# A graph-attention layer on one core: the order of the last blocks' work, and the queue of a path that does not run

## The chip, the core and the metric

The kernel runs on one core of a Trainium2 chip. A core has five engines that run side by side, each from its own queue of instructions: TensorE (matrix products, transposes), VectorE (elementwise work, maxima, searches), ScalarE (activation functions, copies), GpSimd (elementwise work, and here the gathers) and SyncE (starts transfers). Sixteen DMA engines move data between the main memory and the core. Engines and transfers meet in semaphores: an instruction waits until a semaphore has reached a number, and raises another when it is done. The metric is the device's time for one execution in microseconds, the median of several runs. All data are 32-bit floats.

## The reference, cut to what matters

```python
def _L0_gnn_ref(h, adj_mat, W, a):
    N_HEADS, N_HIDDEN, SLOPE = 4, 512, 0.01
    N = h.shape[0]                                             # 4096
    ht = (h @ W).reshape(N, N_HEADS, N_HIDDEN).transpose(1, 0, 2)
    a_src = a[:, :N_HIDDEN, 0]
    a_dst = a[:, N_HIDDEN:, 0]
    src = jnp.einsum('hnd,hd->hn', ht, a_src)
    dst = jnp.einsum('hnd,hd->hn', ht, a_dst)
    e = jax.nn.leaky_relu(src[:, :, None] + dst[:, None, :], SLOPE) + adj_mat[None]
    att = jax.nn.softmax(e, axis=-1)
    h_prime = jnp.einsum('hij,hjd->hid', att, ht)
    return h_prime.mean(axis=0)

x = _layernorm(x + _L0_gnn_ref(x, adj, L0_gnn_W, L0_gnn_a), axis=-1)   # eps 1e-5
```

`x` is 4096 x 512, `adj` 4096 x 4096 (64 MiB), `W` 512 x 2048. The entries of `adj` that are not zero lie between 0.05 and 1e9. They are added to scores of ordinary size, so the softmax of nearly every row is 1 at the row's largest entry of `adj` and 0 elsewhere. Then the attention's result for the row is that one row of `x`, times the mean of the four heads' weights.

## The kernel before

The kernel takes that short way for all rows (`leading_rows`), and beside it tests whether every row's largest entry leads the second by enough. The number of rows for which it doesn't goes into `any_bad`; if it is over zero, a general path computes those blocks in full. With these inputs it is zero, and each engine jumps over the general path at the end.

```python
HINTED = tuple(getattr(mybir.EngineType, name) for name in ("PE", "Activation", "DVE", "Pool"))
# ...
    leading_rows(tc, x, adj, W, a, out, ident, v, n_bad, any_bad)

    flag = nc.values_load(any_bad[0:1, 0:1], min_val=0, max_val=N)
    with tc.If(flag > 0, preferred_fallthrough_block=True, label="general"):
        general(tc, x, adj, W, out, ident, v, n_bad)
```

The 4096 rows are 32 blocks (`NB`) of 128. Each block's rows of `adj` (2 MiB) are loaded, VectorE finds the largest of every 64 entries, then the largest of those and its place; a gather fetches the 64 entries, VectorE finds the column among them, and a second gather fetches that row of `x`. TensorE transposes the gathered rows (`turn`) and multiplies them with the mean weights (`products`); the sum with `x` is normalised by row and stored. `Q` is 4, `LATE` is 28 and `BEHIND` is 24; the `x` rows of blocks 24 to 31 are loaded last, so blocks 24 to 27 get theirs added late (`add_x`). All tasks stand in the program in the order in which each engine runs them.

```python
        nc.vector.max_index(col, top[:, ib, :], adj_t[ib])
        gather_rows(ib, col)

    def turn(ib):
# ...
        tp = psum.tile([P, KB, P], F32, name="tp", bufs=2)
        for kb in range(KB):
            nc.tensor.transpose(tp[:, kb, :], y[:, ts(kb, P)], ident)
        yt = yt_of[ib] = rows.tile([P, KB, P], F32, name="yt")
        nc.scalar.copy(yt, tp)

# ...
    def add_x(engine, ib):
        engine.tensor_add(hold[:, ib, :], hold[:, ib, :], o_ps["by"][:, ib - BEHIND, :])
        o_ps[ib] = hold[:, ib, :]
# ...
    def store(queue, lo, n):
        queue.dma_start(out_rows[:, ds(lo, n), :], hold[:, ds(lo, n), :])
# ...
    def bound(part):

        if part == 0:
            xm = once.tile([P, 1], F32, name="xm")
            nc.vector.tensor_reduce(xm, xx, axis=AX.X, op=OP.max)
            px = of_bound[0] = psum.tile([1, P], F32, name="px", bufs=1)
            nc.tensor.transpose(px, xm, ident)
        elif part == 1:
            nc.vector.tensor_reduce(xg, of_bound[0], axis=AX.X, op=OP.max)
            nc.scalar.activation(xg, xg, AF.Sqrt)
            pb = of_bound[1] = psum.tile([P, 1], F32, name="px", bufs=1)
            nc.tensor.matmul(pb, ones[0:1, :], xg, start=True, stop=True)
        else:
            nc.vector.tensor_mul(lead_by, of_bound[1], vn)
            nc.vector.tensor_scalar(lead_by, lead_by, 1.05, 110.0, op0=OP.mult, op1=OP.add)
# ...
    def test():
        a1 = top[:, :, 0]
        nc.vector.tensor_tensor(gap, top[:, :, 1], inner[:, :, 1], op=OP.max)
        size = once.tile([P, NB], F32, name="size")
        nc.vector.scalar_tensor_tensor(size, a1, -1.0, a1, op0=OP.mult, op1=OP.max)
        nc.vector.tensor_sub(gap, a1, gap)
        nc.vector.tensor_scalar(size, size, -(2.0 ** -22), lead_by, op0=OP.mult, op1=OP.subtract)
        nc.vector.scalar_tensor_tensor(gap, gap, 0.9999, size, op0=OP.mult, op1=OP.add)
        nc.vector.tensor_scalar(gap, gap, 0.0, None, op0=OP.is_gt)

    def count():
        pg = psum.tile([1, NB], F32, name="px", bufs=1)
        nc.tensor.matmul(pg, ones[:, 0:1], gap, start=True, stop=True)
        return pg

    def report(pg):
        nc.vector.tensor_scalar(n_bad, pg, -1.0, float(P), op0=OP.mult, op1=OP.add)
        total = once.tile([1, 1], F32, name="total")
        nc.vector.tensor_reduce(total, pg, axis=AX.X, op=OP.add)
        nc.vector.tensor_scalar(any_bad, total, -1.0, float(N), op0=OP.mult, op1=OP.add)
```

`bound` finds from the largest row norm of `x` how much the first entry has to lead by, `test` compares, `count` adds over the partitions and `report` writes `n_bad` and `any_bad`. `moments` takes mean and variance on VectorE and the root on ScalarE, `factor` the reciprocal, `normalise` the last step on VectorE. `stats`, `rstd` and `finish` do the same on ScalarE and GpSimd.

The loop over the blocks, cut to what the change touches, and the work behind it:

```python
    for t in range(NB):
        if t == NB // 2:
            tc.mark_branch_hint_location("general", engines=HINTED)
        # ... loads, segment maxima, find_column(t - 2)
        if t == NB - 1:
            for ib in (BEHIND, LATE, BEHIND + 2, LATE + 2):
                load_x(ib, 2)
            row_norm(BEHIND)
            row_norm(BEHIND + 1)
            add_x(nc.gpsimd, BEHIND)
        find_segment(t)
        # ... turn(t - 3), products(t - 3), statistics

    row_norm(BEHIND + 2)
    row_norm(BEHIND + 3)
    row_norm(LATE)
    store(nc.sync, 0, Q)
    for ib in range(Q, BEHIND, 2):
        store(nc.sync, ib, 2)
    find_column(NB - 2)
    add_x(nc.gpsimd, BEHIND + 1)
    find_column_in_row(NB - 1)
    add_x(nc.gpsimd, BEHIND + 2)
    turn(NB - 3)
    products(NB - 4, KB - 1, KB)
    residual(NB - 3)
    products(NB - 3)
    for ib in range(LATE + 1, NB):
        row_norm(ib)
    stats(BEHIND)
    moments(LATE)
    bound(0)
    for ib in range(BEHIND, NB):
        find_inner(ib)
    factor(LATE)
    normalise(LATE, o_ps.pop(LATE))
    turn(NB - 2)
    residual_in_halves(NB - 1)
    products(NB - 2, 0, 1)
    bound(1)
    add_x(nc.vector, LATE - 1)
    stats(BEHIND + 1)
    moments(LATE - 1)
    products(NB - 2, 1, KB - 1)
    rstd(slice(BEHIND, BEHIND + 2))
    stats(BEHIND + 2)
    bound(2)
    test()
    pg = count()
    rstd(slice(BEHIND + 2, BEHIND + 3))
    moments(NB - 3)
    factor(LATE - 1, shift=True)
    report(pg)
    factor(NB - 3)
    normalise(NB - 3, o_ps.pop(NB - 3))
    turn(NB - 1)
    finish(BEHIND)
    finish(BEHIND + 1)
    products(NB - 2, KB - 1, KB)
    products_of_half(NB - 1, 0)
    products_of_half(NB - 1, 1)
    nc.vector.tensor_add(hold[:, NB - 2, :], o_ps[NB - 2], hold[:, NB - 2, :])
    o_ps[NB - 2] = hold[:, NB - 2, :]
    moments(NB - 2)
    stats_of_half(NB - 1, 0)
    factor(NB - 2)
    normalise(NB - 2, o_ps.pop(NB - 2))
    finish(BEHIND + 2)
    finish(BEHIND + 3)
    stats_of_half(NB - 1, 1)
    moments(NB - 1)
    factor(NB - 1, shift=True)
    finish_in_halves(NB - 1)
    for ib, n in ((NB - 4, 1), (NB - 3, 1), (BEHIND, 2), (NB - 2, 1), (BEHIND + 2, 2)):
        store(nc.sync, ib, n)
    store(nc.sync, NB - 1, 1)
```

The general path's transfers, all on GpSimd's queue:

```python
        for g in range(NCH):        # 8
            nc.gpsimd.dma_start(x_sb[:, ts(g, Q), :], x_blocks[:, ts(g, Q), :])
        for kb in range(KB):        # 4
            nc.gpsimd.dma_start(w_sb[:, kb, :], w_blocks[:, kb, :])
        # ...
    def block(ib):                  # for each block with a row that does not lead
        # ...
        nc.gpsimd.dma_start(adj_t, adj[ds(ib, P, NB), :])
        # ...
        nc.gpsimd.dma_start(r, x[ds(ib, P, NB), :])
        # ...
        nc.gpsimd.dma_start(out[ds(ib, P, NB), :], r)
```

Of the kernel before, what the change touches and what calls it, by code (L numbers as in the profile page):

```python
# [16 lines left out]
SLOPE = 0.01  # L17
EPS = 1e-5
LOWEST = -3.4028234663852886e38
HINTED = tuple(getattr(mybir.EngineType, name) for name in ("PE", "Activation", "DVE", "Pool"))  # L20
P = 128
C = 512
E = 64
# [43 lines left out]
def leading_rows(ctx, tc, x, adj, W, a, out, ident, v, n_bad, any_bad):  # L67
# [184 lines left out]
    def finish(ib):  # L252
        i = slice(ib, ib + 1)
        nc.scalar.activation(hold[:, ib, :], o_ps.pop(ib), AF.Identity, bias=nm[:, i], scale=sd[:, i])  # L254
# [50 lines left out]
    def store(queue, lo, n):  # L305
        queue.dma_start(out_rows[:, ds(lo, n), :], hold[:, ds(lo, n), :])
# [56 lines left out]
        elif part == 1:  # L363
            nc.vector.tensor_reduce(xg, of_bound[0], axis=AX.X, op=OP.max)
            nc.scalar.activation(xg, xg, AF.Sqrt)
            pb = of_bound[1] = psum.tile([P, 1], F32, name="px", bufs=1)
            nc.tensor.matmul(pb, ones[0:1, :], xg, start=True, stop=True)
        else:
            nc.vector.tensor_mul(lead_by, of_bound[1], vn)
            nc.vector.tensor_scalar(lead_by, lead_by, 1.05, 110.0, op0=OP.mult, op1=OP.add)  # L370

    gap = once.tile([P, NB], F32, name="gap")
# [27 lines left out]
    for t in range(NB):  # L400
# [13 lines left out]
        if t == NB - 1:  # L414
            for ib in (BEHIND, LATE, BEHIND + 2, LATE + 2):
                load_x(ib, 2)
            row_norm(BEHIND)
            row_norm(BEHIND + 1)
            add_x(nc.gpsimd, BEHIND)
        find_segment(t)  # L420
        if t < 2:
            mean_of_heads(t)
# [28 lines left out]
    row_norm(BEHIND + 2)  # L451
    row_norm(BEHIND + 3)
    row_norm(LATE)
    store(nc.sync, 0, Q)
    for ib in range(Q, BEHIND, 2):
        store(nc.sync, ib, 2)
    find_column(NB - 2)
    add_x(nc.gpsimd, BEHIND + 1)
    find_column_in_row(NB - 1)
    add_x(nc.gpsimd, BEHIND + 2)  # L460
    turn(NB - 3)
    products(NB - 4, KB - 1, KB)
    residual(NB - 3)
    products(NB - 3)
    for ib in range(LATE + 1, NB):
        row_norm(ib)
    stats(BEHIND)
    moments(LATE)
    bound(0)
    for ib in range(BEHIND, NB):  # L470
        find_inner(ib)
    factor(LATE)
    normalise(LATE, o_ps.pop(LATE))
    turn(NB - 2)
    residual_in_halves(NB - 1)
    products(NB - 2, 0, 1)
    bound(1)
    add_x(nc.vector, LATE - 1)
    stats(BEHIND + 1)
    moments(LATE - 1)  # L480
    products(NB - 2, 1, KB - 1)
    rstd(slice(BEHIND, BEHIND + 2))
    stats(BEHIND + 2)
    bound(2)
    test()
    pg = count()
    rstd(slice(BEHIND + 2, BEHIND + 3))
    moments(NB - 3)
    factor(LATE - 1, shift=True)
    report(pg)  # L490
    factor(NB - 3)
    normalise(NB - 3, o_ps.pop(NB - 3))
    turn(NB - 1)
    finish(BEHIND)
    finish(BEHIND + 1)
    products(NB - 2, KB - 1, KB)
    products_of_half(NB - 1, 0)
    products_of_half(NB - 1, 1)
# [3 lines left out]
    stats_of_half(NB - 1, 0)  # L502
    factor(NB - 2)
    normalise(NB - 2, o_ps.pop(NB - 2))
    finish(BEHIND + 2)
    finish(BEHIND + 3)
    stats_of_half(NB - 1, 1)
    moments(NB - 1)
# [8 lines left out]
def general(ctx, tc, x, adj, W, out, ident, v, n_bad):  # L517
# [20 lines left out]
    with ExitStack() as pre:  # L538
# [1 line left out]
        two = pre.enter_context(tc.tile_pool(name="two", bufs=2))  # L540
        pps = pre.enter_context(tc.tile_pool(name="pps", bufs=2, space=bass.MemoryType.PSUM))
        for g in range(NCH):
            nc.gpsimd.dma_start(x_sb[:, ts(g, Q), :], x_blocks[:, ts(g, Q), :])
        for kb in range(KB):
            nc.gpsimd.dma_start(w_sb[:, kb, :], w_blocks[:, kb, :])
        for g in range(NCH):
            xT = two.tile([P, KB, C], F32, name="xT")
            for q in range(Q):
# [26 lines left out]
    def block(ib):  # L575
# [1 line left out]
        nc.vector.tensor_copy(src_i, src[:, ds(ib, 1), :].rearrange("p o h -> p (o h)"))  # L577
        held = psum.tile([P, D], F32, name="o_ps", bufs=1)
        adj_t = score.tile([P, N], F32, name="adj_g")
        nc.gpsimd.dma_start(adj_t, adj[ds(ib, P, NB), :])  # L580
        for h in range(H):
            s = score.tile([P, N], F32, name="s")
            nc.scalar.activation(s, dst_b[:, h, :], AF.Identity, bias=src_i[:, h : h + 1])
# [33 lines left out]
                    start=(h == 0 and kb == 0), stop=(h == H - 1 and kb == KB - 1),  # L617
                )
        r = turned.tile([P, D], F32, name="y_g")
        nc.gpsimd.dma_start(r, x[ds(ib, P, NB), :])  # L620
        nc.vector.tensor_add(r, r, held)
        st = stat.tile([P, nc.vector.BN_STATS_DIM], F32, name="st_g")
        nc.vector.bn_stats(st, r)
# [4 lines left out]
        nc.scalar.activation(sd, sd, AF.Sqrt)  # L628
        nc.vector.reciprocal(sd, sd)
        nc.vector.tensor_scalar(r, r, mv[:, 0:1], sd, op0=OP.subtract, op1=OP.mult)  # L630
        nc.gpsimd.dma_start(out[ds(ib, P, NB), :], r)

    with tc.For_i(0, NB, 1) as ib:
        of_block = stat.tile([1, 1], I32, name="of_block", bufs=1)
# [32 lines left out]
```

## Time and profile before

| | |
|---|---|
| time, median of 3 runs | 242.43 us (242.37 to 242.82) |
| span of the profiled run | 240.8 us |
| granted TensorE clock | 0.965 |
| busy: TensorE, VectorE, ScalarE, GpSimd | 83%, 78%, 46%, 42% |
| moved by the DMA engines | 97.73 MB, mean 406 GB/s |
| SyncE's transfers | 88.8% of the DMA engines' span |
| the gathers' transfers | 10.0% |

The span runs from the first to the last recorded instruction; the time on the device is 1.6 us longer. In the profile PE is TensorE, PEld its weight loads, DVE VectorE, ACT ScalarE, POOL GpSimd and SP SyncE; a q behind a name is that engine's queue of control instructions. L208 is line 208 of the kernel. A line of groups shows what is written and read, how often, and the mean time of one; a chain of waits is followed back from the last instruction. The lines that carry the argument are shown in the prediction, under its first heading.

### The profile page before, as it was taken

Reading aid. Unit: us, or ns where it says so; the run is one execution under the profiler, and the core shown is the slowest. Engines: PE = TensorE matmul, PEld = TensorE weight load, DVE = VectorE, ACT = ScalarE, POOL = GpSimd, SP = SyncE. Lnnn points to the kernel's source line nnn. Section 1 sums busy time; section 2 is a strip of 40 time slices with the busy share of each in tenths; the row PEclk is TensorE's granted clock in tenths of the full one; section 3 lists DMA queues with packets and bytes.
Section 4 is the critical chain, followed back from the end, with each engine's and each line's share of the span. In section 5 each row is a group of like instructions: output and inputs, shape, how many; then the busy total and the mean of one; then the engine's idle time right before and its main releaser. Section 6 shows DMA issues by size and latency. Waiting matters only on the chain.

```text
span 240.8 us, 2519 instructions
## 1 busy us (share of the span) xinstructions
PE 199.2 (83%) x683; PEld 102.4 (43%) x683; DVE 186.9 (78%) x308; ACT 111.7 (46%) x267; POOL 100.8 (42%) x215
## 2 busy tenths in 40 slices
PE   0188958999999999999969879597878979979890
PEld 0035426556666655555424334242324433324460
DVE  2635785489869895989589969888799899988682
ACT  2012003035575757575747455446464645157571
POOL 1112322314627362646352753454364564567120
PEclk9999799589999999999999999999997999999997
DMA  6999999999999999999999999999999999999995
GB/s 242 442 419 416 423 429 411 424 416 411 431 410 423 404 425 420 412 413 422 419 423 416 414 422 416 420 407 426 411 430 396 400 398 403 402 410 417 413 385 210
DMA packets 14849, 97.73 MB, mean 406 GB/s; under 512 B 2280, under 2 KB 2280, under 8 KB 9968
## 3 DMA queue, kind: packets, MB, share of 16 engines
q1 hardware_dynamic: 11232, 88.09, 88.8%
q0 software_dynamic: 3584, 9.44, 10.0%
q8 instruction: 6, 0.10, 0.2%
q14 instruction: 11, 0.09, 0.1%
q10 hardware_dynamic: 16, 0.02, 0.0%
HBM read 89.15 MB, written 8.39 MB: 405 GB/s over the span
## 4 chain that ended last, share of the span: by engine, by line
DMA 72%; PE 10%; DVE 6%; issue 4%; POOL 3%; ACT 1%; SPq 1%; POOLq 0%
DMA adj_t<-in_adj_dram 44%; DMA hold<-in_x_dram 18%; PE o L221 5%; DVE seg L158 5%; DMA hold<-in_L_gnn_W_dram 3%; DMA y<-in_x_dram,col 3%; DMA lead<-in_adj_dram,row 3%; PE o L263 1%; PE o L214 1%; PE pv L335 1%; POOL y L181 1%; DVE col L201 1%; SPq L113 1%; PE tp L208 1%; POOL lead L171 1%
## 5 line engine op out<-in xcount | busy, mean ns | idle before, releaser
L158 DVE TENSOR_REDUCE seg<-adj_t 128x32 f32<-128x2048 f32 (+1 forms) x74 | 146.3, 1987 | 38.5 <-DMA adj_t<-in_adj_dram 38.1
L221 PE MATMUL o<-w_sum,yt 128*128 128x512 f32 x248 | 118.2, 618 | 0.7 <-ACT yt L210 0.7
L221 PEld LDWEIGHTS o<-w_sum,yt 128*128 128x128 f32 x248 | 45.7, 196 | 55.1 <-issue 44.0
L210 ACT COPY yt<-tp 128x512 f32<-128x512 f32 x32 | 18.8, 588 | 44.3 <-PE tp L208 38.3
L171 POOL DMA_INDIRECT lead<-in_adj_dram,row x32 | 32.3, 1008 | 14.1 <-POOL row L169 14.1
L181 POOL DMA_INDIRECT y<-in_x_dram,col x32 | 30.8, 963 | 15.7 <-POOL col L195 14.6
L208 PE MATMUL tp<-ident,y 128*128 128x128 f32 x128 | 19.7, 277 | 15.5 <-DMA y<-in_x_dram,col 15.5
L311 PE MATMUL o<-hold,ident 128*128 128x512 f32 x32 | 18.7, 737 | 15.7 <-DMA hold<-in_L_gnn_W_dram 15.7
L214 PE MATMUL o<-hold,ident 128*128 128x512 f32 x52 | 27.7, 615 | 1.2 <-DMA hold<-in_x_dram 1.2
L208 PEld LDWEIGHTS tp<-ident,y 128*128 128x128 f32 x128 | 14.3, 141 | 28.9 <-issue 27.5
L195 POOL TENSOR_TENSOR col<-start,within 128x1 uint32<-128x1 uint32 x31 | 5.9, 189 | 48.0 <-DVE within L193 48.0
L329 ACT COPY wt<-tp 128x512 f32<-128x512 f32 x16 | 9.2, 588 | 35.7 <-PE tp L327 35.7
L169 POOL TENSOR_TENSOR row<-at,first 128x1 uint32<-128x1 uint32 x32 | 6.0, 188 | 38.3 <-DVE at L167 38.3
L228 ACT ACTIVATE sq<-hold 128x512 f32<-128x512 f32 x32 | 19.8, 621 | 4.3 <-DMA hold<-in_x_dram 4.3
L335 PEld LDWEIGHTS pv<-at_d,wt 128*128 128x128 f32 x128 | 17.2, 200 | 7.3 <-ACT wt L329 3.7
L311 PEld LDWEIGHTS o<-hold,ident 128*128 128x128 f32 x32 | 7.3, 239 | 24.8 <-POOL row L169 11.0
L254 ACT ACTIVATE hold<-o,nm,sd 128x512 f32<-128x512 f32 x24 | 17.3, 775 | 0.0
L312 ACT ACTIVATE w_sum<-o 128x512 f32<-128x512 f32 x4 | 2.4, 598 | 31.8 <-PE o L311 31.8
L245 ACT ACTIVATE sq<-o,nm 128x512 f32<-128x512 f32 x24 | 16.5, 689 | 0.8
L335 PE MATMUL pv<-at_d,wt 128*128 128x2 f32 x128 | 16.0, 249 | 0.6 <-ACT wt L329 0.6
L243 ACT ACTIVATE sq<-o 128x512 f32<-128x512 f32 x24 | 14.7, 611 | 0.0
L327 PEld LDWEIGHTS tp<-ident,hold 128*128 128x128 f32 x64 | 7.9, 142 | 6.9 <-issue 6.9
(85 smaller groups left out, 137.3 us busy)
## 6 DMA issues: line engine op xcount, KB each, us to landing
adj_t<-in_adj_dram SPq DMA_DIRECT2D x27, 2048.0 KB
adj_t<-in_adj_dram SPq DMA_DIRECT2D x20, 512.0 KB
hold<-in_x_dram SPq DMA_DIRECT2D x6, 1024.0 KB
out_dram<-hold SPq DMA_DIRECT2D x12, 512.0 KB
hold<-in_L_gnn_W_dram SPq DMA_DIRECT2D x4, 1024.0 KB
hold<-in_x_dram SPq DMA_DIRECT2D x4, 512.0 KB
out_dram<-hold SPq DMA_DIRECT2D x1, 1024.0 KB
out_dram<-hold SPq DMA_DIRECT2D x4, 256.0 KB
```

The lines of the kernel that those rows point to most:

```text
L158: nc.vector.tensor_reduce(seg_of[ib][:, ts(k, S // n)], adj_t[ib][:, ts(k, N // n)].rearrange("p (s e) -> p s e", e=E), axis=AX.X, op=OP.max,)
L171: nc.gpsimd.indirect_dma_start(out=lead, out_offset=None, in_=adj_segs, in_offset=bass.IndirectOffsetOnAxis(ap=row[:, :1], axis=0),)
L181: nc.gpsimd.indirect_dma_start(out=y, out_offset=None, in_=x, in_offset=bass.IndirectOffsetOnAxis(ap=col[:, :1], axis=0),)
L208: nc.tensor.transpose(tp[:, kb, :], y[:, ts(kb, P)], ident)
L210: nc.scalar.copy(yt, tp)
L214: nc.tensor.matmul(o_ps[ib], ident, hold[:, ib, :], start=True, stop=False)
L221: nc.tensor.matmul(o_ps[ib], yt_of[ib][:, kb, :], w_sum[:, kb, :], start=(start and kb == 0), stop=(kb == KB - 1),)
L228: nc.scalar.activation(sq, hold[:, ib, :], AF.Square, accum_out=xx[:, ib : ib + 1])
L245: nc.scalar.activation(sq, o, AF.Square, bias=nm[:, i], accum_out=sd[:, i])
L254: nc.scalar.activation(hold[:, ib, :], o_ps.pop(ib), AF.Identity, bias=nm[:, i], scale=sd[:, i])
L311: nc.tensor.matmul(o, ident, hold[:, w_at + kb * H + h, :], start=(h == 0), stop=(h == H - 1))
L335: nc.tensor.matmul(pv[:, kb, h : 2 * H : H], wt[:, k, :], at_d[:, k, h : 2 * H : H], start=(k == 0), stop=(k == KB - 1),)
```

## The change

It does four things. The last tasks of the five engines get another order: the bound and the test come earlier against the work of the last four blocks, and one addition on GpSimd is moved behind a gather. The stores of the first 24 blocks are cut otherwise: ten of two blocks and then one of four, where one of four came first. The general path's transfers go to SyncE's queue instead of GpSimd's. And SyncE is told of the branch over the general path ahead of time, as the four other engines are. It is for an earlier end of the test and of the last block, and for a GpSimd queue without transfers in the general path.

```diff
-HINTED = tuple(getattr(mybir.EngineType, name) for name in ("PE", "Activation", "DVE", "Pool"))
+HINTED = tuple(getattr(mybir.EngineType, name) for name in ("PE", "Activation", "DVE", "Pool", "SP"))
@@ bound(part)
             nc.scalar.activation(xg, xg, AF.Sqrt)
-            pb = of_bound[1] = psum.tile([P, 1], F32, name="px", bufs=1)
+        elif part == 2:
+            pb = of_bound[2] = psum.tile([P, 1], F32, name="px", bufs=1)
             nc.tensor.matmul(pb, ones[0:1, :], xg, start=True, stop=True)
         else:
-            nc.vector.tensor_mul(lead_by, of_bound[1], vn)
+            nc.vector.tensor_mul(lead_by, of_bound[2], vn)
@@ the loop, t == NB - 1
             row_norm(BEHIND + 1)
-            add_x(nc.gpsimd, BEHIND)
         find_segment(t)
@@ behind the loop
-    store(nc.sync, 0, Q)
-    for ib in range(Q, BEHIND, 2):
+    for ib in range(0, BEHIND - Q, 2):
         store(nc.sync, ib, 2)
+    store(nc.sync, BEHIND - Q, Q)
     find_column(NB - 2)
+    add_x(nc.gpsimd, BEHIND)
     add_x(nc.gpsimd, BEHIND + 1)
     find_column_in_row(NB - 1)
     add_x(nc.gpsimd, BEHIND + 2)
     turn(NB - 3)
     products(NB - 4, KB - 1, KB)
     residual(NB - 3)
-    products(NB - 3)
+    products(NB - 3, 0, KB - 1)
     for ib in range(LATE + 1, NB):
         row_norm(ib)
     stats(BEHIND)
     moments(LATE)
     bound(0)
+    products(NB - 3, KB - 1, KB)
     for ib in range(BEHIND, NB):
         find_inner(ib)
+    bound(1)
     factor(LATE)
     normalise(LATE, o_ps.pop(LATE))
     turn(NB - 2)
     residual_in_halves(NB - 1)
-    products(NB - 2, 0, 1)
-    bound(1)
+    bound(2)
+    products(NB - 2, 0, 2)
+    bound(3)
+    test()
+    pg = count()
+    products(NB - 2, 2, KB - 1)
     add_x(nc.vector, LATE - 1)
     stats(BEHIND + 1)
+    stats(BEHIND + 2)
     moments(LATE - 1)
-    products(NB - 2, 1, KB - 1)
     rstd(slice(BEHIND, BEHIND + 2))
-    stats(BEHIND + 2)
-    bound(2)
-    test()
-    pg = count()
     rstd(slice(BEHIND + 2, BEHIND + 3))
+    report(pg)
+    turn(NB - 1)
     moments(NB - 3)
     factor(LATE - 1, shift=True)
-    report(pg)
     factor(NB - 3)
     normalise(NB - 3, o_ps.pop(NB - 3))
-    turn(NB - 1)
-    finish(BEHIND)
-    finish(BEHIND + 1)
+    for ib in range(BEHIND, BEHIND + 3):
+        finish(ib)
     products(NB - 2, KB - 1, KB)
@@ ... normalise(NB - 2), then
-    finish(BEHIND + 2)
     finish(BEHIND + 3)
@@ general(), and the same in its four other transfers
-            nc.gpsimd.dma_start(x_sb[:, ts(g, Q), :], x_blocks[:, ts(g, Q), :])
+            nc.sync.dma_start(x_sb[:, ts(g, Q), :], x_blocks[:, ts(g, Q), :])
```

More of the change, by code (lines that the diff above doesn't have):

```diff
@@ L542, in general @@
         for g in range(NCH):
-            nc.gpsimd.dma_start(x_sb[:, ts(g, Q), :], x_blocks[:, ts(g, Q), :])
+            nc.sync.dma_start(x_sb[:, ts(g, Q), :], x_blocks[:, ts(g, Q), :])
         for kb in range(KB):
-            nc.gpsimd.dma_start(w_sb[:, kb, :], w_blocks[:, kb, :])
+            nc.sync.dma_start(w_sb[:, kb, :], w_blocks[:, kb, :])
         for g in range(NCH):
@@ L579, in block @@
         adj_t = score.tile([P, N], F32, name="adj_g")
-        nc.gpsimd.dma_start(adj_t, adj[ds(ib, P, NB), :])
+        nc.sync.dma_start(adj_t, adj[ds(ib, P, NB), :])
         for h in range(H):
@@ L619, in block @@
         r = turned.tile([P, D], F32, name="y_g")
-        nc.gpsimd.dma_start(r, x[ds(ib, P, NB), :])
+        nc.sync.dma_start(r, x[ds(ib, P, NB), :])
         nc.vector.tensor_add(r, r, held)
@@ L630, in block @@
         nc.vector.tensor_scalar(r, r, mv[:, 0:1], sd, op0=OP.subtract, op1=OP.mult)
-        nc.gpsimd.dma_start(out[ds(ib, P, NB), :], r)
+        nc.sync.dma_start(out[ds(ib, P, NB), :], r)
     with tc.For_i(0, NB, 1) as ib:
```

## The prediction, made before the result was known

> **What bounds the kernel now.** I read the page first, then the stretches of the last 16 us, then the chain of work that ended last, then the waits of single engines near the end, and last the records of the branch. The page says that the 16 DMA engines are full from the second slice to the last but one:
>
> ```profile
> PE   0188958999999999999969879597878979979890
> DVE  2635785489869895989589969888799899988682
> DMA  6999999999999999999999999999999999999995
> DMA packets 14849, 97.73 MB, mean 406 GB/s; under 512 B 2280, under 2 KB 2280, under 8 KB 9968
> ```
>
> 97.73 MB at about 410 GB/s is some 238 us of the 240.8 us span. The change moves the same bytes, so it can win or lose only at the ends. The stretches of 2 us show where there is room (columns: stretch, its length, each engine's busy time, granted clock, DMA share, GB/s):
>
> ```profile
> 230.00:232.00 2.00, 2.00 (x11) 1.29 (x10) 1.89 (x9) 1.59 (x4) 0.76 (x3) 1.00 1.02 413
> 232.00:234.00 2.00, 2.00 (x11) 1.77 (x10) 1.77 (x6) 1.42 (x4) 0.00 (x0) 1.00 0.88 338
> 234.00:236.00 2.00, 1.07 (x5) 0.58 (x4) 1.09 (x3) 1.18 (x3) 0.00 (x0) 1.00 0.92 361
> 236.00:238.00 2.00, 0.00 (x0) 0.00 (x0) 0.78 (x3) 0.68 (x2) 0.00 (x0) 0.86 0.73 293
> 238.00:240.00 2.00, 0.00 (x0) 0.00 (x0) 0.00 (x0) 0.00 (x0) 0.00 (x0) 0.50 0.37 140
> ```
>
> The DMA engines lack work for 2 x (0.12 + 0.08 + 0.27 + 0.63) = 2.2 us, nearly all of it after 232. Up to there the backlog of stores hides everything; behind it the last block's arithmetic sets the end. The chain of waits gives its parts (start, length, what):
>
> ```profile
> 217.25 7.90 DMA y<-in_x_dram,col
> 225.28 0.63 PE tp L208 x4
> 225.91 0.87 PE o L259 x4
> 227.71 0.31 PE px L367 x2
> 229.93 0.15 PE px L386 x2
> 230.08 0.59 PE tp L208 x4
> 231.53 3.55 PE o L263 x16
> 235.10 0.44 DVE halves_st L297
> 236.53 0.57 ACT hold L303
> ```
>
> The 7.90 us is the gather for block 30, but the second L208 group belongs to block 31, whose gather has landed at about 227.3 by the DMA records: its transposes stand 2.8 us behind other TensorE work. From their start to the last ScalarE write is 237.10 - 230.08 = 7.0 us. In this stretch VectorE waits once for long, for the matmul of the bound, and SyncE waits for a normalisation:
>
> ```profile
> DVE lead_by L369 <- PE px L367: 1.7, 1, 1.7
> SPq L306 <- DVE hold L290: 8.5, 3, 5.6
> ```
>
> Last, the branch over the general path (queue, operation, count, length in ns, first and last start):
>
> ```profile
> L62 POOLq EVENT_SEMAPHORE  x5: 17/42/43, 231.9 to 232.2; - x5
> L62 POOLq INC_SWDGE_SEM  x1: 1472/1472/1472, 232.3 to 232.3; - x1
> L62 SPq COMPARE_BRANCH  x1: 50/50/50, 238.4 to 238.4; - x1
> L62 SPq EVENT_SEMAPHORE  x1: 17/17/17, 238.6 to 238.6; - x1
> L662 SPq EVENT_SEMAPHORE  x14: 17/28/28, 238.7 to 240.8; - x14
> ```
>
> GpSimd, which issues the general path's transfers, waits behind its branch for its eight transfer semaphores and raises them by what the skipped transfers would have added. SyncE has one such step. Then SyncE runs twelve waits in a row, 0.06 us apart (238.65, 238.72 ... 239.28); the twelfth, for the last store, is over at 239.91. The barriers behind it end at 240.8.
>
> [...] a store on the other path: issued at 237.13, awaited until 239.91, 2.8 us for 256 KB. [...] No such wait is seen on SyncE, which goes on 0.13 us after its branch; on the three announced engines ScalarE, VectorE and GpSimd it takes 0.4 to 0.5 us. [...] here it is 50 to 84 ns on those engines and SyncE, so the branch itself is nothing.
>
> **The change, part by part.**
>
> *The announcement.* Each announced engine runs a hint of 50 to 55 ns at 0.93 to 1.05 us. On ScalarE the first transfer starts 0.09 us later than SyncE's, behind its hint. SyncE's first load would start about 0.07 us later, at the head of a stream that never runs dry. Cost +0.07 us.
>
> *The last gathers.* The addition of 1.27 us on GpSimd (start 213.96) goes behind block 30's gather. VectorE's index for block 31 is there at 214.31, so the row sum starts at 214.4 instead of 215.19; but block 30's column then waits behind the gather of 0.97 us, and its own gather starts near 216.7 instead of 217.25. It lands about 0.5 us earlier, near 224.6. Block 31's gather stays at 220.65, as it waits for the search that ends at 219.89.
>
> *TensorE's order.* The transpose for the bound goes ahead of two matmuls of block 29 (0.9 us). Those end near 224.5, so block 30's transposes can start at 224.6 (before 225.28). They take 0.63 and the halves' residuals 0.87: 226.1. The bound's matmul is ready there, as its square root now precedes block 30's copy on ScalarE; VectorE goes on 0.4 us later, at 226.5, instead of 228.06. The test takes 229.37 - 228.06 = 1.3 us: 227.8. The count follows 0.5 us later as now, ends at 228.5, two more matmuls of block 30 take 0.9, and block 31's transposes start at 229.3 to 229.6, not 230.08. With the 5.0 us from there to TensorE's end (235.08 - 230.08), TensorE is done 0.5 to 0.8 us sooner.
>
> *VectorE's order takes that back.* The addition and moments of block 27, 1.6 us, now fill VectorE's wait (224.78 to 226.39). After the change they stand behind the test: 227.8 + 1.65 = 229.45. Then the report 0.4, moments of block 29 0.9, two factors of block 27 0.4: 231.1. The root for block 29 stands behind block 31's copy on ScalarE, so its normalisation starts near 231.4, not 230.90. From there: normalise 0.72, add block 30 0.72, its moments 0.9, first half's statistics 0.45, factor 0.15 and normalise 0.6: the second half's statistics start at 231.4 + 3.55 = 234.95 against 235.10 now. If the bound's matmul comes 0.4 us later than I put it, they start at 235.35. So the last store is issued between 0.15 us earlier and 0.3 us later: +0.1 us.
>
> *The stores.* Bytes and count are the same; the transfer of 1 MB goes from first to eleventh of the early group. Eight are in flight at all times, which is enough either way. Block 29's store comes 0.5 us later, into the stretch where the DMA engines already lack work. I put this into the +0.1.
>
> *The general path's transfers.* None of them runs. But the repair of semaphores behind the branch follows the engine that owns the transfers, so it moves to SyncE. There the eight semaphores are those of the stores themselves. SyncE would stop at the last store's semaphore, until about 239.9, in that repair, and only then run the twelve waits that are hidden under the store's landing today: 12 x 0.06 = 0.7 us behind it. GpSimd loses its 1.47 us step, which lies at 232.3 and on no path. I take 0.6 us, for some doubt that all twelve come behind.
>
> Sum: 0.07 + 0.1 + 0.6 = 0.8 us on 242.43: **243.2 us**.
>
> **The rivals.**
>
> *The reorder wins and the repair costs nothing.* TensorE's early transposes speak for it: if VectorE keeps up, the last store goes out 0.5 us earlier, and the DMA gap after 232 leaves room. For it speaks that block 31's rows are there at 227.3. Against it is VectorE's load. This gives 241.9 to 242.2.
>
> *SyncE's branch waits for instructions.* The path to be skipped grows by 15 transfer instructions with their waits[...].
>
> *Everything is hidden by the DMA engines.* With the same bytes and a backlog up to 232, the end stays within 0.2 us: 242.4. The empty DMA time after 232 and the serial waits at the end speak against it.
>
> **Range and chances.** The repair on SyncE is the largest term, and I give it three chances in four; the order of work is worth half a microsecond in either direction; a late instruction fetch has one chance in ten. That gives 242.2 to 244.3 for eight in ten. Two per cent is 4.8 us, more than twice the 2.2 us of empty DMA time at the end, and more than any loss above: faster 0.01, same 0.97, slower 0.02.
>
> **What would show it.** On SyncE's queue eight or nine semaphore steps at the branch's line instead of one, and the row of final waits behind the last landing: the span's end 1.6 us behind that landing, not 0.95. At the start, one hint on SyncE. Block 31's transposes near 229.5, VectorE's wait for the bound over near 226.5, and no long VectorE wait ahead of the second half's statistics. The prediction is wrong if the final waits still run under the landing, if SyncE's branch is followed by more than 0.6 us of nothing, or if the last ScalarE write comes more than 0.5 us off 237.1.

## The result, and the profile after

The changed kernel took 244.07 us (median of six runs, 243.12 to 244.40), the kernel before on the same chip 242.53 (six runs, 242.34 to 243.01). The ratio is 1.0053, with a 95% interval of 1.0030 to 1.0075: half a per cent slower, well under the 2% that the prediction names. The same program measured again later, beside other kernels (further down), took 243.38 against 242.49, ratio 1.0043 (1.0028 to 1.0058). Predicted were 243.2, and 242.2 to 244.3.

The page's three lines on the whole execution:

```profile
span 242.3 us, 2523 instructions
DMA  6999999999999999999999999999999999999984
GB/s 225 400 418 425 429 419 415 421 423 410 426 415 412 413 423 421 421 409 420 421 421 417 417 422 417 408 418 423 413 424 396 402 398 406 398 409 414 423 356 191
```

The span is 242.3 us, not 240.8. The DMA engines are as full as before, except in the second slice, which moved 400 GB/s where the kernel before moved 442. That is looked at below, as no part of the change but the announcement stands so early.

The branch's line and the kernel's end in the changed kernel (queue, operation, count, shortest, median and longest in ns, first and last start in us):

```profile
L62 SPq EVENT_SEMAPHORE  x9: 17/17/17, 239.6 to 240.6; - x9
L62 POOLq EVENT_SEMAPHORE  x1: 17/17/17, 232.5 to 232.5; - x1
```

```profile
L664 SPq EVENT_SEMAPHORE  x14: 17/28/28, 240.7 to 242.2; - x14
```

GpSimd's five steps have become one and its step of 1.47 us is gone; SyncE's one step has become nine. Each of the eight further ones waits for one of the eight semaphores that SyncE's transfers raise, and raises it (by how much, the trace doesn't tell), at 239.66, 239.75 ... 240.59. The last of the nine waits for the last store. It was issued at 237.71 and the wait ended at 240.59. Only then come the twelve final waits, from 240.66 to 241.33, and the barriers, to 242.2. From the landing to the end of the span are 1.7 us; before they were 0.9.

The chain of waits in the changed kernel (start, length, what), and below it VectorE's longest wait near the end (total, times, longest):

```profile
226.09 0.44 PE tp L208 x4
...
227.39 0.31 PE px L368 x2
...
229.61 0.15 PE px L387 x2
...
230.82 0.45 PE tp L208 x4
...
235.77 0.36 DVE halves_st L297
...
237.12 0.57 ACT hold L303
```

```profile
DVE lead_by L370 <- PE px L368: 1.3, 1, 1.3
```

The last ScalarE write stands at 237.12 where it was 236.53, and that looks like a loss in the last arithmetic. It is none: from its first 10 us on, the DMA engines of this execution are behind. By the time at which 20 to 85 MB had been moved they are 0.75 us later than in the kernel before, and 237.12 - 0.75 = 236.4 is a little earlier than 236.53. Times with this lag taken off are called "by the stream" below. Where the lag comes from, the repetition of the kernel shows.

### The profile page after: what moved, and what is told of

Same layout as the page of the kernel before. It is cut to its first block, busy times and chain, and to the rows that moved or that the text cites. A ratio compares the mean times of both kernels' runs of the same rounds, so it can differ in the third digit from the quotient of the medians.

```text
span 242.3 us, 2523 instructions
## 1 busy us (share of the span) xinstructions
PE 196.4 (81%) x683; PEld 100.8 (42%) x683; DVE 186.7 (77%) x308; ACT 111.9 (46%) x267; POOL 101.6 (42%) x215
## 4 chain that ended last, share of the span: by engine, by line
issue 36%; POOL 33%; DMA 19%; PE 5%; DVE 4%; ACT 1%; POOLq 1%; SPq 1%
DMA adj_t<-in_adj_dram 16%; POOL lead L171 11%; POOL y L181 10%; POOL sd L249 4%; DMA y<-in_x_dram,col 3%; PE o L221 3%; POOL start L176 2%; POOL col L195 2%; POOL row L169 2%; DVE seg L158 2%; POOL sd L248 1%; POOL nm L250 1%; PE tp L208 1%; SPq L113 1%; POOLq L181 0%
## 5 line engine op out<-in xcount | busy, mean ns | idle before, releaser
L221 PE MATMUL o<-w_sum,yt 128*128 128x512 f32 x248 | 115.6, 606 | 0.7 <-ACT yt L210 0.7
L221 PEld LDWEIGHTS o<-w_sum,yt 128*128 128x128 f32 x248 | 44.7, 192 | 53.6 <-issue 42.8
L311 PE MATMUL o<-hold,ident 128*128 128x512 f32 x32 | 19.5, 764 | 17.9 <-DMA hold<-in_L_gnn_W_dram 17.9
L214 PE MATMUL o<-hold,ident 128*128 128x512 f32 x52 | 27.6, 614 | 0.6 <-DMA hold<-in_x_dram 0.6
L335 PEld LDWEIGHTS pv<-at_d,wt 128*128 128x128 f32 x128 | 16.3, 191 | 6.8 <-ACT wt L329 3.5
L335 PE MATMUL pv<-at_d,wt 128*128 128x2 f32 x128 | 15.3, 244 | 0.6 <-ACT wt L329 0.6
L249 POOL TENSOR_TENSOR sd<-sd,power 128x2 f32<-128x2 f32 (+1 forms) x14 | 10.5, 749 | 1.2
```

Of the source, the lines that this page charges most:

```text
L214: nc.tensor.matmul(o_ps[ib], ident, hold[:, ib, :], start=True, stop=False)
L221: nc.tensor.matmul(o_ps[ib], yt_of[ib][:, kb, :], w_sum[:, kb, :], start=(start and kb == 0), stop=(kb == KB - 1),)
L249: nc.gpsimd.tensor_tensor(sd[:, i], sd[:, i], power[:, : i.stop - i.start], op=OP.pow)
L311: nc.tensor.matmul(o, ident, hold[:, w_at + kb * H + h, :], start=(h == 0), stop=(h == H - 1))
L335: nc.tensor.matmul(pv[:, kb, h : 2 * H : H], wt[:, k, :], at_d[:, k, h : 2 * H : H], start=(k == 0), stop=(k == KB - 1),)
```

## The experiments

Two theories stood after this. **A**: the repair of semaphores on SyncE is the cost, some 0.7 us, and the order of work is worth nothing. **B**: something else that the change adds, either the announcement and what it does to the first loads, or the new order of work, costs as much again. All kernels were timed beside the kernel before; each ratio is to that kernel in the same group of runs (242.38, 242.40 and 242.49 us, on three chips).

**The general path's transfers on SyncE's queue, alone.** The kernel before with five edits of this kind:

```diff
-        nc.gpsimd.dma_start(adj_t, adj[ds(ib, P, NB), :])
+        nc.sync.dma_start(adj_t, adj[ds(ib, P, NB), :])
```

> The kernel before with the general path's transfers on SyncE and nothing else. Theory (repair on SyncE): eight semaphore steps more at the branch on SyncE, the twelve final waits behind the last landing, span's end 1.6 us behind that landing instead of 0.95; time +0.7 us (243.1 to 243.3). Rival (the loss is in the order of work and in a slower start of the loads, the repair hides under the landing): time within 0.2 us of before. Rival (late instruction fetch without the announcement): more than 0.6 us between SyncE's branch and its next step[...].

It took 243.08 us (19 runs, 242.84 to 244.06), ratio 1.0028 (1.0018 to 1.0038): 0.70 us more. The branch's line and the kernel's end in this kernel:

```profile
L62 SPq EVENT_SEMAPHORE  x9: 17/17/17, 238.6 to 239.5; - x9
```

```profile
L662 SPq EVENT_SEMAPHORE  x14: 17/28/28, 239.6 to 241.1; - x14
```

The last store landed at 239.52, and the end of the span stands 1.7 us behind it. With nothing else changed, that is the predicted repair and its predicted size. SyncE's branch, which nobody announced here, was over at 238.19, and the next step came at 238.64, 0.45 us later. In the changed kernel, with the announcement, these are 239.11 and 239.56: the same 0.45. Before the change it was 0.13. So the branch over the longer path costs SyncE 0.3 us more, announced or not, and they lie under the landing of the last store.

**The announcement alone.** The kernel before with one name more:

```diff
-HINTED = ... ("PE", "Activation", "DVE", "Pool"))
+HINTED = ... ("PE", "Activation", "DVE", "Pool", "SP"))
```

> The kernel before with the branch announced to SyncE too, nothing else. Theory (the announcement costs only its own 0.06 us ahead of the first load): +0.05 to +0.1 us. Rival (the announcement disturbs SyncE's first issues, which is the 1 us that the loads lost between 4 and 8 us in the changed kernel): +0.5 to +1 us, SyncE's issues of 0.7 to 1.1 us at 3 to 6 us as there.

It took 242.68 us (22 runs, 242.2 to 243.4), ratio 1.0013 (1.0005 to 1.0021): 0.1 to 0.5 us more, where 0.07 were predicted. The instruction that announces it lasts 0.06 us, and SyncE's first load starts 0.11 us later than in the kernel before (in the trace of the changed kernel 0.20 us behind the opening barrier, in that of the kernel before 0.08). ScalarE's load of `a` now goes first, which SyncE's loads did before.

**The announcement, with that load out of the way.** As the last kernel, with the loads of `a` issued by GpSimd:

```diff
-    for s in range(2):
-        nc.scalar.dma_start(a_rows[ts(s, H), :], ...)
     ...
     nc.gpsimd.memset(eps, EPS)
+    for s in range(2):
+        nc.gpsimd.dma_start(a_rows[ts(s, H), :], ...)
```

> The kernel before with the announcement to SyncE, and the two small loads of a moved from ScalarE's queue to GpSimd's, behind its constants, so that no transfer of ScalarE is issued ahead of SyncE's first load. Theory (what costs is the flip of the first two issues): the first issues take 0.33 to 0.5 us each, the moved bytes 20 us in are as in the kernel before, time within 0.1 us of before. Rival (the announcement itself disturbs SyncE): issues of 0.7 us and more at 3 to 6 us and +0.3 us as with the announcement alone.

It took 242.64 us (21 runs, 242.35 to 243.67), ratio 1.0003 (0.9992 to 1.0014). The two together leave the announcement a cost between nothing and half a microsecond; whether the order of the first issues makes the difference is not settled by two intervals that overlap.

**The new order of work and of the stores, alone.** The changed kernel with the general path's transfers back on GpSimd's queue and without the announcement:

```diff
-HINTED = ... ("PE", "Activation", "DVE", "Pool", "SP"))
+HINTED = ... ("PE", "Activation", "DVE", "Pool"))
 ...
-        nc.sync.dma_start(adj_t, adj[ds(ib, P, NB), :])
+        nc.gpsimd.dma_start(adj_t, adj[ds(ib, P, NB), :])
```

> The changed order of work and of the stores alone; the general path's transfers on GpSimd as before, no announcement. Theory: set against the loads' stream the last store went out 0.4 us earlier in the changed kernel, so this is 0.3 to 0.5 us faster than before, 242.0 to 242.2. The prediction's own sum for this part was +0.1, which gives 242.5. Rival (the new order of the stores slows the stream): +0.5 us or more.

It took 242.48 us (14 runs, 242.09 to 244.18), ratio 0.9999 (0.9978 to 1.0020). The order is worth nothing that these runs can tell from zero, with half a microsecond of doubt either way.

**A better order of VectorE's work.** The prediction had said that VectorE takes back what TensorE wins, because block 27's addition no longer fills its wait for the bound. This kernel is the last one with that repaired:

```diff
     normalise(LATE, o_ps.pop(LATE))
+    add_x(nc.vector, LATE - 1)
     turn(NB - 2)
     residual_in_halves(NB - 1)
     bound(2)
-    products(NB - 2, 0, 2)
+    stats(BEHIND + 1)
+    moments(LATE - 1)
     bound(3)
     test()
+    products(NB - 2, 0, KB - 1)
     pg = count()
-    products(NB - 2, 2, KB - 1)
-    add_x(nc.vector, LATE - 1)
-    stats(BEHIND + 1)
     stats(BEHIND + 2)
-    moments(LATE - 1)
     rstd(slice(BEHIND, BEHIND + 2))
     rstd(slice(BEHIND + 2, BEHIND + 3))
-    report(pg)
-    turn(NB - 1)
     moments(NB - 3)
+    turn(NB - 1)
     factor(LATE - 1, shift=True)
+    report(pg)
```

> The changed order alone (general path on GpSimd, no announcement), mended: the addition and the moments of block 27 come back into VectorE's wait for the bound, the count behind three products of block 30, the report behind the moments of block 29. Theory (in the changed order VectorE's list was what took back TensorE's lead): the last store goes out 0.5 to 0.7 us earlier than before, time 241.8 to 242.1. Rival (the last 256 KB store lands when the DMA engines are through with the others, whatever comes earlier): within 0.15 us of before.

It took 242.56 us (13 runs, 242.15 to 243.28), ratio 1.0000 (0.9982 to 1.0018). In its trace the last store was issued at 236.93 and awaited until 240.10. The last issue came 0.2 us before that of the kernel before, and it bought nothing.

**The general path's transfers on ScalarE's queue.** If the repair goes with the engine that issues, ScalarE, which waits for no store at the end, would hide it. The changed kernel without the announcement, and:

```diff
-        nc.sync.dma_start(adj_t, adj[ds(ib, P, NB), :])
+        nc.scalar.dma_start(adj_t, adj[ds(ib, P, NB), :])
```

> The changed order of work, the general path's transfers on ScalarE's queue instead of SyncE's, no announcement to SyncE. Theory (what costs is that SyncE does the repair and the final list one after the other, behind the last landing): ScalarE repairs while SyncE goes through its list, so 242.0 to 242.3, with the span's end about 1 us behind the last landing. Rival (a repair of these eight semaphores costs 0.7 us wherever it stands, since the barrier waits for it): 242.7 to 243.0.

It took 243.69 us (12 runs, 242.84 to 245.05), ratio 1.0048 (1.0032 to 1.0065). The branch's line in this kernel:

```profile
L62 SPq EVENT_SEMAPHORE  x9: 17/17/17, 238.3 to 240.5; - x9
...
L62 ACTq EVENT_SEMAPHORE  x2: 17/17/17, 237.2 to 237.3; - x2
```

The nine steps stand on SyncE still, though SyncE issues none of the skipped transfers; ScalarE has its two, as in the other kernels. So my picture of the repair was wrong in one point: it does not follow the issuing engine. With GpSimd's queue the repair was on GpSimd, as four further steps and the one of 1.47 us; with either of the other two it is on SyncE, as eight further steps. SyncE's branch was over at 238.17 here and the next step came at 238.30, 0.13 us later as in the kernel before: the 0.3 us more go with the transfers that SyncE jumps over, not with the nine steps.

**The changed kernel without the announcement.**

```diff
-HINTED = ... ("PE", "Activation", "DVE", "Pool", "SP"))
+HINTED = ... ("PE", "Activation", "DVE", "Pool"))
```

> The changed kernel without the announcement to SyncE: new order, general path's transfers on SyncE. Theory (the announcement flips which engine issues the first transfer and the loads then lose up to 1 us in the first 8 us; the repair costs 0.7; the order nothing that can be measured): 243.0 to 243.2, and SyncE's first issues all of 0.33 to 0.5 us. Rival (the early loss is chance of an execution): 244, as the changed kernel. Rival (without the announcement SyncE waits for instructions behind its branch): more than 0.6 us between the branch and the next step.

It took 243.70 us (7 runs, 243.05 to 245.49), ratio 1.0049 (1.0035 to 1.0064). The announcement saves nothing that shows, as SyncE's 0.45 us behind the branch said. The profiled execution was the slowest of the seven, and its trace shows something that no theory had. SyncE's last stores in it (five issues; shortest, median, longest), and the DMA engines in the same time (columns as in the prediction):

```profile
L306 SPq DMA_DIRECT2D out_dram<-hold x5: 332/332/1936, 233.7 to 238.2; - x5
```

```profile
232.00:234.00 2.00, 2.00 (x9) 1.41 (x8) 1.77 (x7) 2.00 (x5) 0.18 (x1) 1.00 0.52 207
234.00:236.00 2.00, 2.00 (x10) 1.54 (x9) 1.85 (x6) 1.50 (x3) 0.00 (x0) 1.00 0.42 147
...
238.00:240.00 2.00, 0.00 (x0) 0.00 (x0) 0.04 (x1) 0.19 (x1) 0.00 (x0) 1.00 1.02 392
```

One issue took 1.94 us where the others take 0.33: the store of blocks 24 and 25, at 234.08, directly behind the store of block 29. In those 4 us the DMA engines lacked work for 2 x (0.48 + 0.58) = 2.1 us, and what they had not done stood at the end: full again at 238 to 240, the last store issued at 238.21 and awaited until 242.03. The ScalarE-queue kernel has the same, an issue of 1.91 us in the same place.

In the old order each of the five late stores was issued at least 0.2 us behind the end of the issue ahead, as `finish(BEHIND)` and the other finishes became ready one by one. In the new order blocks 24 and 25 are ready before block 29, and SyncE issues the two stores back to back. Over the traces, behind 12 us, an issue that follows another by over 0.4 us takes 0.33 to 0.35 us (some 57 in each; in two kernels a single one took longer, 0.55 and 0.62). One that follows by less than 0.1 us mostly takes 0.37 to 0.73, and in three kernels one took 1.35 to 1.94. That made a third theory, **C**: the back-to-back issue is part of the cost. The next kernels take it away, and add it.

**The late stores of blocks 24 to 27 issued by ScalarE.** The kernel without the announcement, with two of its five late stores on ScalarE's queue, right behind the work that makes them ready:

```diff
-    for ib in range(BEHIND, BEHIND + 3):
-        finish(ib)
+    finish(BEHIND)
+    finish(BEHIND + 1)
+    store(nc.scalar, BEHIND, 2)
+    finish(BEHIND + 2)
 ...
     finish(BEHIND + 3)
+    store(nc.scalar, BEHIND + 2, 2)
 ...
-    for ib, n in ((NB - 4, 1), (NB - 3, 1), (BEHIND, 2), (NB - 2, 1), (BEHIND + 2, 2)):
+    for ib, n in ((NB - 4, 1), (NB - 3, 1), (NB - 2, 1)):
```

> The new order with the general path's transfers on SyncE, no announcement, and the stores of blocks 24-25 and 26-27 issued by ScalarE right behind the work that writes them, so that SyncE's last stores no longer stand back to back. Theory (with that order SyncE issues a store within 0.1 us of the one before, the issue then takes up to 1.9 us, and the bunched stores land late): no late SyncE issue over 0.35 us, time 243.0 to 243.2 (before + the repair's 0.7), against 243.7 for the same without this. Rival (the width comes from somewhere else): 243.6 or more.

It took 243.06 us (22 runs, 242.80 to 243.74), ratio 1.0019 (1.0009 to 1.0029). The late stores in this kernel:

```profile
L306 SPq DMA_DIRECT2D out_dram<-hold x3: 332/332/332, 231.7 to 236.2; - x3
...
L306 ACTq DMA_DIRECT2D out_dram<-hold x2: 382/388/395, 232.1 to 234.3; - x2
```

No issue is long now, and the interval lies below that of the kernel without this edit (1.0035 to 1.0064): 0.7 us less by the ratios. This is for C, but it does not prove it: the edit also moves these two stores to another engine's queue, and the two kernels ran on different chips. What is left, about 0.5 us, is no more than the repair's own 0.7.

**Back-to-back issues added to the kernel before.** Four of its late stores cut into two of 64 partitions each:

```diff
-    for ib, n in (... (NB - 3, 1), (BEHIND, 2), (NB - 2, 1), (BEHIND + 2, 2)):
-        store(nc.sync, ib, n)
+        for part in (slice(0, P // 2), slice(P // 2, P)) if ib != NB - 4 else ...:
+            nc.sync.dma_start(out_rows[part, ds(ib, n), :], hold[part, ds(ib, n), :])
```

> The kernel before with the stores of block 29, 24-25, 30 and 26-27 each cut into two of 64 partitions, issued one right after the other: same bytes and same pieces of 2 or 4 KB. Theory (an issue back to back can take long, and that delays the end): issues over 0.38 us in the last 10 us, time +0.2 to +0.6 us and a wider spread. Rival (back to back is harmless in itself): within 0.15 us of before.

It took 245.11 us (6 runs, 244.06 to 246.69), ratio 1.0106 (1.0071 to 1.0140). Its last nine stores on SyncE, and one stretch:

```profile
L513 SPq DMA_DIRECT2D out_dram<-hold x9: 333/554/1351, 225.9 to 237.6; - x9
```

```profile
234.00:236.00 2.00, 1.62 (x8) 1.09 (x6) 1.31 (x4) 1.55 (x3) 0.00 (x0) 1.00 0.96 246
```

Half of the issues took 0.55 us or more, one 1.35, and the whole cost 2.6 us. But this run does not separate two things: in the stretch the DMA engines are busy for 0.96 of the time and move only 246 GB/s, where the kernel before moved 361 at 0.92. So the transfers themselves took longer for their bytes. It shows that such a cut is costly, and does not show that the issues are why.

**The better order, and ScalarE's stores.** The kernel with the mended VectorE order, general path on GpSimd, and the two stores on ScalarE's queue as above:

```diff
+    store(nc.scalar, BEHIND, 2)
 ...
+    store(nc.scalar, BEHIND + 2, 2)
```

> The mended order with the general path on GpSimd, no announcement, and the two late stores issued by ScalarE. Theory (its last store went out 0.5 us earlier, and what was left of the gain was lost in stores issued back to back): 241.9 to 242.2. Rival (the end is set by the DMA engines that have 1.8 MB of late stores to move): 242.3 to 242.5 as before.

It took 242.36 us (14 runs, 242.21 to 243.12), ratio 0.9999 (0.9987 to 1.0010). Its last store was issued at 236.94, was awaited until 239.91, and the end came where it was. This is against C in its plain form: in these kernels without the repair on SyncE the back-to-back issue is worth nothing that shows, whether there or not, with half a microsecond of doubt.

**The repair and the announcement, without the new order.** The kernel before, with the general path on SyncE's queue and `"SP"` announced:

```diff
+HINTED = ... ("PE", "Activation", "DVE", "Pool", "SP"))
 ...
+        nc.sync.dma_start(adj_t, adj[ds(ib, P, NB), :])
```

> The kernel before with the general path's transfers on SyncE and the announcement, without the new order. If the two costs add, 242.4 + 0.7 + 0.3 = 243.4. If the announcement takes something off the repair (a quicker step behind the branch), 243.1 or less. If the announcement costs 0.8 us once SyncE's path is long, 243.9, the changed kernel's time without any part for the order.

It took 243.34 us (6 runs, 243.05 to 243.68), ratio 1.0038 (1.0025 to 1.0050). Against the same without the announcement that is 0.0010 more, 0.24 us, with intervals that overlap.

**The changed kernel once more**, with no edit.

> The changed kernel as it is, beside the others on one chip. Sum of the parts as measured alone: 242.4 + 0.7 (repair) + 0.25 (announcement) + 0 to 0.1 (order) = 243.3 to 243.5. If the parts hurt each other, as the first measurement says: 243.8 to 244.2.

It took 243.38 us (13 runs, 242.95 to 244.65), as given at the top. The stretches of 3 us at the start, first in the first trace of the changed kernel, then in this one:

```profile
3.00:6.00 3.00, 0.00 (x0) 0.00 (x0) 1.46 (x2) 0.00 (x0) 0.00 (x0) 1.00 0.96 341
6.00:9.00 3.00, 0.00 (x0) 0.00 (x0) 1.48 (x2) 0.00 (x0) 0.00 (x0) 1.00 1.02 347
```

```profile
3.00:6.00 3.00, 0.00 (x0) 0.00 (x0) 1.61 (x2) 0.00 (x0) 0.00 (x0) 1.00 1.01 403
6.00:9.00 3.00, 0.00 (x0) 0.00 (x0) 2.62 (x3) 0.00 (x0) 0.00 (x0) 1.00 1.04 426
```

The same program moved 341 and 347 GB/s in one execution and 403 and 426 in the other. In the 20 us behind SyncE's first issue it moved 7.24 MB and 7.62 MB; the kernel before moved 7.62. The 0.38 MB are 0.9 us at 410 GB/s, the lag that the first trace had against this one between 20 and 85 MB. So the same program has it in one execution and not in another; whether the change makes it more frequent, one trace of each kernel doesn't show. SyncE's issues at 2.76 to 6.31 us show it too: first trace, then this one.

```profile
2.76 0.73 SPq L119 DMA_DIRECT2D hold<-in_L_gnn_W_dram  x1
...
4.51 1.07 SPq L113 DMA_DIRECT2D adj_t<-in_adj_dram  x1
5.63 0.68 SPq L119 DMA_DIRECT2D hold<-in_L_gnn_W_dram  x1
```

```profile
2.76 0.45 SPq L119 DMA_DIRECT2D hold<-in_L_gnn_W_dram  x1
...
4.31 0.47 SPq L113 DMA_DIRECT2D adj_t<-in_adj_dram  x1
4.82 0.45 SPq L119 DMA_DIRECT2D hold<-in_L_gnn_W_dram  x1
```

A guess of mine in between, that it comes from ScalarE's load going first, fell: this trace has ScalarE's load first and no loss, and the kernel without the announcement has SyncE's first and 7.41 MB.

This execution was the fastest of its thirteen (242.95 us), and its trace shows how far the new order can go. Its chain and the stretches of its end:

```profile
228.70 0.45 PE tp L208 x4
...
233.66 0.36 DVE halves_st L297
...
235.00 0.57 ACT hold L303
```

```profile
234.00:236.00 2.00, 0.00 (x0) 0.00 (x0) 0.99 (x5) 0.86 (x2) 0.00 (x0) 1.00 0.93 371
236.00:238.00 2.00, 0.00 (x0) 0.00 (x0) 0.00 (x0) 0.00 (x0) 0.00 (x0) 0.58 0.83 327
```

SyncE's last five stores and its nine steps (count; shortest, median, longest; first and last start), and, at the end, the last five stores in the kernel before:

```profile
L306 SPq DMA_DIRECT2D out_dram<-hold x5: 332/333/382, 231.0 to 235.6; - x5
L62 SPq EVENT_SEMAPHORE  x9: 17/17/17, 237.4 to 239.5; - x9
```

```profile
L306 SPq DMA_DIRECT2D out_dram<-hold x5: 332/332/332, 231.7 to 237.1; - x5
```

All arithmetic is over at 235.57, not 237.10, and the last store is issued at 235.59 instead of 237.13. Its landing moved from 239.91 to 239.49 only. This trace is 0.14 us ahead of the kernel before by the stream, so the issue came 1.4 us earlier and the landing 0.3. The store waited 3.90 us, not 2.78, because the DMA engines were still busy with the stores ahead of it; they are at 0.83 of their time for 2 us after the last engine has stopped.

## Why the prediction was right, and where it was not

Steps from the kernel before to the changed one, from the ratios above, each difference of ratios times 242.4 us:

```
before -> general path on SyncE                         +0.68   (1.0028)
       -> with the announcement                         +0.24   (1.0038)
       -> with the new order = changed kernel           +0.12   (1.0043)
or
before -> general path on SyncE                         +0.68   (1.0028)
       -> with the new order                            +0.51   (1.0049)
       -> with the announcement = changed kernel        -0.15   (1.0043)
```

The first step is clear of the noise. The 0.51 is so by little (0.1 to 0.9, an estimate from the two intervals), and the other three are not.

**The repair on SyncE: right, and so was its size.** The prediction took 0.6 of a possible 0.7 us. Measured alone it is 0.7 (0.4 to 0.9), with the nine steps, the stop at the last store's semaphore and the twelve waits behind it. That it "follows the engine that owns the transfers" is wrong, as ScalarE's queue showed; for this change it makes no difference.

**The announcement: right that it is small.** Predicted +0.07. Alone it measured 0.1 to 0.5 us, with the loads of `a` moved -0.2 to 0.3, and on top of the whole change nothing. More than "0 to 0.5 us" can't be said. The rival in which SyncE's branch waits for instructions lacks the sign that the prediction had named, more than 0.6 us of nothing behind the branch: it is 0.45 us, with the announcement and without. That is 0.3 us more than before, under the last landing, and what fills it is not shown; nor did any trace show how long a wait of that kind would be.

**TensorE's order: the gain depends on the execution.** By the stream, block 31's transposes came at 230.82 - 0.75 = 230.1 in the first trace, no earlier than before (230.08), and at 228.70 + 0.14 = 228.8 in the repetition, on either side of the 229.3 to 229.6 foreseen. With the order alone and with the kernel without the announcement they came at 230.9 and 231.1; in these two traces the granted clock was 0.5 for 3.4 us from 214 us on, and a group of transposes there took 1.09 us instead of 0.63. VectorE's wait for the bound was to be over near 226.5; it was over at 227.0 and 225.8, and still lasted 1.3 us. (Block 31's rows were all there at 227.85 in the kernel before, not at about 227.3; its transposes stood behind other work all the same.)

**VectorE takes it back: right in the first trace, wrong in the repetition.** The second half's statistics were to start at 234.95; by the stream they started at 235.77 - 0.75 = 235.0 and at 233.66 + 0.14 = 233.8. The last ScalarE write of the repetition ended at 235.57, more than the 0.5 us off 237.1 that the prediction had named as a sign of being wrong.

**The last store's issue sets the end: wrong.** This is the step that failed. I counted each tenth of a microsecond on that issue as one on the end. In the repetition the issue came 1.4 us earlier and the landing 0.3. The other traces say the same. By the stream, eleven of the fourteen, all but the three with an issue of 1.35 us or more, issue their last store between 235.7 and 237.8 and have it landed between 239.6 and 240.2: over 2 us of difference at the issue are 0.6 us at the landing. Three kernels with a new order and without the repair on SyncE show ratios of 0.9999, 1.0000 and 0.9999. The rival that everything is hidden by the DMA engines is right for the order of work; its counterargument, the 2.2 us of empty DMA time behind 232, overlooked that the late stores' 1.8 MB must pass in any case.

**Missing from the sum: SyncE's stores issued back to back.** I saw that the stores' order changes and took "eight in flight at all times" as the whole of it (in the kernel before, SyncE's stores from 207.2 to 223.7 us are each issued 0.05 us after a wait for the transfer eight places ahead). Where SyncE also has the repair, the new order measured 0.1 us with the announcement and 0.5 without, and moving two stores to ScalarE took 0.7 off the latter. Without the repair it measured nothing, within half a microsecond. Why it counts in one place and not in the other, and what makes some of these issues last 1.9 us, stays open.

That the sum of 0.8 us came near the 0.9 to 1.5 measured is therefore the merit of one term; that a small cost for the order and one for the announcement came out about right, for other reasons than the ones given, is luck.

## What to carry to other kernels

Look at what a skipped branch leaves behind: none of its transfers ran here, and still eight semaphores of transfers were waited for and raised behind it, one by one from 239.66 to 240.61 us in the changed kernel. On SyncE that cost 0.70 us by itself, as the last of the eight is the last store's and the twelve final waits come behind it; such work belongs on an engine that does not wait for this store. Which engine gets it has to be looked up in the trace: of the three queues tried here, only GpSimd's kept it off SyncE. Where the DMA engines still have a backlog, an earlier last issue may hardly move the landing: in the repetition they were at 0.83 of their time for 2 us behind the last arithmetic, and an issue 1.4 us earlier brought the landing forward by 0.3 us. Before an early difference between two traces is explained, run one of the kernels again: here the same program differed by 0.9 us from its first 10 us on.

## What the runs showed of the hardware that was not expected

- The wait for the last 256 KB store lasted 2.4 to 4.3 us from its issue (2.42 with the general path on SyncE and announced, 2.78 before, 3.90 in the repetition, 4.11 with the general path on ScalarE's queue, 4.31 behind the halved stores). In the repetition the DMA engines were at 0.83 of their time from 236 to 238 us, behind the last arithmetic; in the kernel before, from 237.1 to 239.1, at 0.53.
- Behind the first 12 us, SyncE's issue of a transfer took 0.33 to 0.35 us with a pause of over 0.4 us ahead of it (some 57 in each trace; 0.55 and 0.62 once each, in two of them), mostly 0.37 to 0.73 with one of less than 0.1 us, and in three traces one took 1.35 to 1.94 us.
- Behind its branch over the general path SyncE went on after 0.13 us in the kernel before, and after 0.45 us with the general path's transfers on its queue, announced or not; with the transfers on ScalarE's queue it was 0.13 us again.
